# A four-layer attention and mixture-of-experts kernel: order of work in the second attention, and when the overflow slots run

## The chip, the cores and the metric

One core of a Trainium2 chip runs the whole program. Its engines work side by side, each through its own instructions in order: TensorE (PE in the profile, its weight loads PEld), VectorE (DVE), ScalarE (ACT), GpSimd (POOL), and SyncE (SP), which here only issues transfers. TensorE writes to PSUM; VectorE and ScalarE read it. The metric is the device time of one execution in microseconds (us), lower is better; the median of the runs is compared.

## The reference

Eight sequences of 256 tokens with 256 features pass four residual layers. The first mixes by correlation, the second is a balanced mixture of eight experts. The change touches the third and fourth:

```python
def _L1_xattn_ref(x, data, Wq, bq, Wkv, bkv, Wp, bp):
    ...
    q = (x @ Wq + bq).reshape(bs, n_ctx, HEADS, d)
    kv = (data @ Wkv + bkv).reshape(bs, n_data, HEADS, 2 * d)
    k, v = (kv[..., :d], kv[..., d:])
    scores = jnp.einsum('bqhd,bkhd->bhqk', q, k) * scale
    attn = jax.nn.softmax(scores, axis=-1)
    out = jnp.einsum('bhqk,bkhd->bqhd', attn, v).reshape(bs, n_ctx, WIDTH)
    return out @ Wp + bp

def _L1_ffn_ref(hidden_states, gate_W, w1_e, w3_e, w2_e, w1_s, w3_s, w2_s):
    ...
    probs = jax.nn.softmax(logits, axis=-1)
    top_v, top_i = jax.lax.top_k(probs, K)        # K = 2 of E = 8 experts
    g = jax.nn.silu(jnp.einsum('td,edf->etf', flat, w1_e))
    u = jnp.einsum('td,edf->etf', flat, w3_e)
    out_e = jnp.einsum('etf,efd->etd', g * u, w2_e)
    routed = jnp.einsum('te,etd->td', gates, out_e).reshape(b, s, d)
    ...                                           # and a shared expert
    return alpha * shared + (1.0 - alpha) * routed

x = x + _L1_xattn_ref(_layernorm(x, axis=-1), ctx_1024, ...)
x = x + _L1_ffn_ref(_layernorm(x, axis=-1), ...)
```

Everything is in float32: B = 8 sequences (called batches), S = 256 tokens, D = 256 features, 16 heads of 16, F = 1024 hidden features.

## The kernel before

Tokens lie on the 128 partitions, two tiles of 128 for a batch (TPB = 2); features are in two halves of 128 (KC = 2, and NB = 2 groups of eight heads). The whole program is written out in one order: each engine executes its instructions in the order in which the code issues them, and waits come from the tiles that they read and write.

**The second attention** (lines 2968 to 3054) runs over (b, c): batch b, group of heads c. One step holds two sets of `scores` (one for each 128 keys, `kt` 0 and 1). Each set is four products into two PSUM buffers of 128x1024 (pool `ps_s`, two buffers) and two exponentials on ScalarE that empty them. `values` of the step before are multiplied between the first and the second set, and `keep` copies them out on VectorE. Work of other batches is put between these:

- `turn_q(b+1)`, c = 0: turns the normalised rows of the next batch by four TensorE transpositions, and VectorE copies them from PSUM to `hT`.
- `queries(b+1, c)`: four products of `hT`, then two copies of the result into `QM`, each with one half of the heads masked out: the first on ScalarE, the second on VectorE.
- `turn_back(b-1)`: transposes the kept values, and VectorE divides by the sums of the softmax.
- `add_y(b+2)`, `batch_stats(b+2, "q")`: the residual and the statistics of a later batch. The statistics run on VectorE; the inverse root (`pow` and four small operations) on POOL.
- `turn_out(b-1)`, `project_out(b-1)`, c = 1: the output product and residual of the batch before. `norm_q(b+2)` normalises a later batch, one tile on VectorE and, from b = 2 on, the other on POOL; `add_bias` runs on POOL.
- `batch_stats(b-2, "m")`, `norm_m(b-2)`, c = 0: normalise the finished rows for the fourth layer; the normalisation is two POOL instructions. `turn_m(b-2)`, c = 1, turns them.

Copies to and from PSUM of all helpers share the pool `ps_m` with three buffers.

**The router** is the generator `route(g)` for four tiles (two batches): its pieces are issued one by one by `next(gates)`, three times in each (b, c), from batch 4 on. Piece 1 (issued when it is made) computes the logits; 2 turns them and takes the exponential on ScalarE; 3 to 5 pick the two largest on VectorE; 6 counts by two products with a triangular matrix and ones; 7 sums the counts (VectorE, `run`, line 2868); 8 yields the addresses. `send()` then scatters one row tile for one choice by an indirect transfer of POOL; sends wait for one another.

**The fourth layer** runs over blocks of 512 tokens: two shared blocks, eight experts, one shared. A block consists of four up units and one down unit (`run_unit`), on TensorE some 40 us. An expert takes its first 512 rows; more rows go to four slots of 32 rows (`slots()`, line 3616), a generator of which one piece is issued after most up units (`next(beside)`). It goes through F in four quarters (`q`): in one piece the way up (32 products of 32 columns each, line 3652, silu and product), in the next two transpositions, in the third the way down (16 products, line 3672) and, through `load_slots(q + 1)`, the transfers of the next quarter's weights: eight for the way up, four for the way down, 256 KB each, issued by SP. The piece with the last quarter's way down also loads the shared weights of the last block (`WS`). Between blocks, SP issues the weights of the experts and, in `take_apart` (line 3524), the transposing transfers of the rows of a block to come, which `join` (line 3530) puts together on ScalarE.

Of the kernel before, what the change touches and what calls it, by code (L numbers as in the profile page):

```python
# [19 lines left out]
P = 128  # L20
# [1066 lines left out]
def fast_path(  # L1087
# [1502 lines left out]
    def norm_q(b, *engs):  # L2590
        h2s[b] = hn.tile([P, TPB, D], F32, tag="h4", name="h2")
        batch_norm(b, "q", h2s[b], engs)
# [8 lines left out]
    def turn_pair(src, dst, copy):  # L2601
# [5 lines left out]
                )  # L2607
        copy(dst, pt.rearrange("p k j q -> p k (j q)"))

    def turn_q(b):  # L2610
        hTs[b] = pq2.tile([P, KC, S], F32, tag="hT", name="hT")
        turn_pair(h2s.pop(b), hTs[b], nc.vector.tensor_copy)

    def queries(b, c):
        if c == 0:
            QM[b] = pq2.tile([P, NB, 2, S], F32, tag="QM", name="QM")
        pp = ps_m.tile([P, S], F32, tag="pm", name="pp")
        for kc in range(KC):
            nc.tensor.matmul(
                pp,  # L2620
                wq[:, kc, c * P : (c + 1) * P],
                hTs[b][:, kc, :],
                start=(kc == 0),
                stop=(kc == KC - 1),
            )
        nc.scalar.activation(
            QM[b][:, c, 0, :],
            pp,
            AF.Identity,
            bias=bqm[:, c, 0:1],  # L2630
            scale=mask[:, 0:1],
        )
        nc.vector.tensor_scalar(
            QM[b][:, c, 1, :],
            pp,
            mask[:, 1:2],
            bqm[:, c, 1:2],
            ALU.mult,
            ALU.add,
        )  # L2640

    pex = at.enter_context(tc.tile_pool(name="pex", bufs=4))
    ex, pvs, ovs, ons, oTs = {}, {}, {}, {}, {}
# [305 lines left out]
        list(vals(i, 2, ps_m))  # L2949
    norm_q(0, nc.vector, nc.vector)  # L2950
    hTs[0] = pq2.tile([P, KC, S], F32, tag="hT", name="hT")
    transpose_tokens(h2s[0], hTs[0], ps_m, "pm", 0)
    nc.vector.tensor_tensor(bpb, bpb, pbp, ALU.add)
    queries(0, 0)
    queries(0, 1)
# [12 lines left out]
    for b in range(B):  # L2968
        for c in range(NB):
            scores(b, c, 0)  # L2970
            if (b, c) == (3, 0):
                router_weights()
            if prev:
                values(*prev, 0)
                values(*prev, 1)
                keep(*prev)
            send()
            if gates:
                next(gates, None)
            if prev is None:  # L2980
                list(vals(4, 1, ps_m, nc.vector.tensor_copy))
            elif b == 0:
                turn_q(1)
                norm_q(2, nc.vector, nc.vector)
                queries(1, 0)
                queries(1, 1)
            elif c == 0:
                if b + 1 < B:
                    turn_q(b + 1)
            else:  # L2990
                turn_out(b - 1)
                if 2 < b + 2 < B:
                    norm_q(b + 2, nc.vector, nc.vector if b < 2 else nc.gpsimd)
                    add_bias(b + 2)
            scores(b, c, 1)
            if gates:
                next(gates, None)
            if c == 0 and b >= 2:
                batch_stats(b - 2, "m")
                norm_m(b - 2)  # L3000
            send()
            if gates:
                next(gates, None)
            if c == 0:
                if b >= 1:
                    turn_back(b - 1)
                if 0 < b and b + 1 < B:
                    queries(b + 1, 0)
                    queries(b + 1, 1)
                if b + 2 < B and b:  # L3010
                    add_y(b + 2)
                    batch_stats(b + 2, "q")
                if b >= 4 and b % 2 == 0:
                    gates = route(b // 2 - 2)
                    next(gates)
            else:
                if b >= 2:
                    turn_m(b - 2)
                if b >= 1:
                    project_out(b - 1)  # L3020
                else:
                    add_bias(2)
            if prev is None:
                list(vals(5, 1, ps_m, nc.vector.tensor_copy))
                ct_scope.close()
                wsp = ctx.enter_context(tc.tile_pool(name="wsp", bufs=1, side="right"))
                pg1 = ctx.enter_context(tc.tile_pool(name="pg1", bufs=1, side="right"))
# [24 lines left out]
            if (b, c) == (1, 0):  # L3052
                router_columns()
            prev = b, c
# [4 lines left out]
    NQ = 4  # L3059
# [537 lines left out]
            for g in range(SLOTS)  # L3597
        ]

    def load_slots(q):  # L3600


        fs = slice(q * FQ, (q + 1) * FQ)
        wab = wsp.tile([P, 2, SLOTS, KC, FQ], F32, tag="wab", name=f"sab_{q}")
        wc = wsp.tile([P, SLOTS, FQ // P, D], F32, tag="wc", name=f"sc_{q}")
        wa, wb = wab[:, 0], wab[:, 1]
        for w, src in ((wa, L1_ffn_w1_e), (wb, L1_ffn_w3_e), (wc, L1_ffn_w2_e)):
            for g, e in enumerate(experts):
                part = src[bass.ds(e, 1)]
                part = part[:, fs, :] if w is wc else part[:, :, fs]  # L3610
                nc.sync.dma_start(
                    out=w[:, g], in_=part.rearrange("o (c p) d -> p (o c) d", p=P)
                )
        return wa, wb, wc

    def slots():

# [5 lines left out]
            in_=Td,  # L3623
            in_offset=bass.IndirectOffsetOnAxis(ap=rows_u, axis=0),
        )
        w = load_slots(0)
        yield
        gate = pg1.tile([P, 1], F32, name="gate")
        junk = pg1.tile([P, E], F32, name="junk")
# [14 lines left out]
        nc.vector.tensor_copy(RT, pt)  # L3644
        yield
        py = ps_v.tile([P, D], F32, tag="pv", name="pys")
        for q in range(NQ):
            pgu = ps_m.tile([P, 2, FQ], F32, tag="pm", name="pgu")
            for i in range(2):
                for kc in range(KC):  # L3650
                    for g in range(SLOTS):
                        nc.tensor.matmul(
                            pgu[g * SR : (g + 1) * SR, i, :],
                            RT[:, kc, g * SR : (g + 1) * SR],
                            w[i][:, g, kc, :],
                            start=(kc == 0),
                            stop=(kc == KC - 1),
                            skip_group_check=True,
                        )
            a = pe2.tile([P, FQ], F32, tag="as", name="as", bufs=1)  # L3660
            nc.scalar.activation(a, pgu[:, 0, :], AF.Silu)
            nc.vector.tensor_tensor(a, a, pgu[:, 1, :], ALU.mult)
            yield
            pt = ps_m.tile([P, FQ // P, P], F32, tag="pm", name="pt")
            for fi in range(FQ // P):
                nc.tensor.transpose(pt[:, fi, :], a[:, fi * P : (fi + 1) * P], ident)
# [3 lines left out]
            for fi in range(FQ // P):  # L3670
                for g in range(SLOTS):
                    nc.tensor.matmul(
                        py[g * SR : (g + 1) * SR, :],
                        aT[:, fi, g * SR : (g + 1) * SR],
                        w[2][:, g, fi, :],
                        start=(q == 0 and fi == 0),
                        stop=(q == NQ - 1 and fi == FQ // P - 1),
                        skip_group_check=True,
                    )
            if q + 1 < NQ:  # L3680
                w = load_slots(q + 1)
            else:
                WS = load_l1(wsp, -1)
                Y = pe2.tile([P, D], F32, tag="Ys", name="Ys", bufs=1)
                nc.scalar.activation(Y, py, AF.Copy, scale=gate)
                for g in range(SLOTS):
                    add_rows(Y[g * SR : (g + 1) * SR, :], ids[:, g : g + 1])
# [252 lines left out]
```

## Time and profile before

| | |
|---|---|
| runs, us | 823.51, 822.27, 825.11, 822.15 |
| median, us | 822.89 |
| profiled execution, us | 820.12 |
| its span, first to last instruction, us | 818.4 |
| granted TensorE clock | 0.999 |
| transfers | 109.59 MB, mean 134 GB/s |

The page gives the busy time and its share of the span for each engine. A timeline row holds: start from the beginning of the span, duration of the merged group, engine, line, operation, tile written and tiles read, shape, number of instructions, and in brackets the idle time of the engine before it with what ended it. Busy time by stretches, in us:

| stretch | length | PE | DVE | ACT | POOL |
|---|---|---|---|---|---|
| 200 to 222 | 22 | 21.22 | 6.10 | 7.17 | 3.06 |
| 222 to 238 | 16 | 13.64 | 10.50 | 10.25 | 5.93 |
| 238 to 254 | 16 | 16.00 | 8.13 | 10.65 | 3.86 |
| 286 to 302 | 16 | 15.33 | 13.08 | 11.17 | 8.38 |
| 302 to 318 | 16 | 14.51 | 10.53 | 9.12 | 9.98 |
| 318 to 334 | 16 | 16.00 | 9.78 | 11.57 | 8.29 |
| 334 to 350 | 16 | 15.76 | 7.49 | 6.65 | 10.59 |
| 510 to 530 | 20 | 20.00 | 13.30 | 9.38 | 4.68 |

The second attention lies from 222 to 342 us, the slots' products from 515 to 651 us.

### The profile page before, as it was taken

What the parts mean: (1) busy time and instruction counts of PE and PEld (TensorE: products, weight loads), DVE (VectorE), ACT (ScalarE), POOL (GpSimd) and SP (SyncE); (2) the same over time, 40 slices, a digit from 0 to 9 for tenths busy, and PEclk for the clock granted to TensorE, in tenths of its full rate; (3) what the DMA queues carried; (4) which work ended last, traced back from release to release, by engine and by line L of the source; (5) the groups of instructions that cost most, each with busy time, mean ns of one, the idle gap of its engine ahead of it and who ended that gap; (6) DMA issues with size and microseconds to landing.
All of it is one profiled execution on the core that took longest, in us unless ns stands there. A gap on an engine that the chain in (4) does not pass through costs nothing. (4 is left out here: it accounts for less than half of the span.)

```text
span 818.4 us, 13790 instructions
## 1 busy us (share of the span) xinstructions
PE 793.9 (97%) x5124; PEld 627.9 (77%) x5124; DVE 519.0 (63%) x1470; ACT 361.9 (44%) x672; POOL 216.7 (26%) x293
## 2 busy tenths in 40 slices
PE   8999999999999999999999999999999999999997
PEld 7546688778745555556899989797979798999986
DVE  6378877340456686555785777767676759586731
ACT  4344454324366666532334454444444544433330
POOL 6352122131125455552330000202020322112030
PEclk9999999999999999999999999999999999999999
DMA  8395567942160000142223485394949495411023
GB/s 264 90 289 177 170 202 224 323 156 91 42 178 27 15 1 24 38 164 90 71 69 79 132 261 156 84 297 96 287 100 302 90 317 113 136 14 20 7 40 120
DMA packets 104724, 109.59 MB, mean 134 GB/s; under 512 B 26408, under 2 KB 95240, under 8 KB 104616
## 3 DMA queue, kind: packets, MB, share of 16 engines
q1 hardware_dynamic: 95976, 95.30, 38.0%
q0 software_dynamic: 7920, 13.02, 7.4%
q8 instruction: 42, 0.69, 0.4%
q10 hardware_dynamic: 752, 0.30, 0.1%
q14 instruction: 34, 0.28, 0.1%
HBM read 80.61 MB, written 25.37 MB: 129 GB/s over the span
## 5 line engine op out<-in xcount | busy, mean ns | idle before, releaser
L3536 POOL DMA_INDIRECT Od<-Y,ids x32 | 51.8, 1620 | 291.7 <-DVE Y L3361 100.1
L3221 ACT COPY B<-a 128x512 f32<-128x512 f32 (+1 forms) x54 | 28.6, 531 | 169.7 <-PE a L3233 133.7
L2660 ACT ACTIVATE ex<-p,scale 128x1024 f32<-128x1024 f32 x64 | 67.8, 1111 | 32.5 <-PE p L2652 31.7
L3233 PE MATMUL a<-T,HP 128*128 128x256 f32 x288 | 73.9, 379 | 0.0
L3233 PE MATMUL a<-RT,wab 128*128 128x256 f32 x256 | 66.7, 383 | 0.4 <-DVE cc L3083 0.4
L3083 DVE TENSOR_TENSOR cc<-e,s 128x512 f32<-128x512 f32 x44 | 30.4, 690 | 57.6 <-PE e L3233 57.6
L3083 DVE TENSOR_TENSOR act<-act 128x256 f32<-128x256 f32 (+1 forms) x120 | 61.4, 512 | 2.7
L2372 PE MATMUL ph<-RT,w 128*128 128x256 f32 x256 | 61.7, 389 | 0.8 <-ACT RT L2359 0.7
L2389 PE MATMUL py<-w,A 128*128 128x256 f32 x256 | 61.6, 388 | 0.0
L3233 PEld LDWEIGHTS a<-T,HP 128*128 128x128 f32 x288 | 54.0, 190 | 7.0
L2381 ACT ACTIVATE A<-ph,b1c 128x256 f32<-128x256 f32 x64 | 30.1, 473 | 53.9 <-PE ph L2372 46.6
L3233 PEld LDWEIGHTS a<-RT,wab 128*128 128x128 f32 x256 | 46.3, 190 | 9.2 <-DVE cc L3083 2.5
L2372 PEld LDWEIGHTS ph<-RT,w 128*128 128x128 f32 x256 | 45.3, 190 | 8.9 <-ACT A L2381 1.1
L2389 PEld LDWEIGHTS py<-w,A 128*128 128x128 f32 x256 | 46.6, 190 | 6.4
L2894 POOL DMA_INDIRECT Td<-HP,to x32 | 32.6, 1018 | 56.4 <-DMA Td<-HP,to 48.9
L2652 PE MATMUL p<-QM,KT 32*128 32x512 f32 x256 | 40.4, 640 | 1.7 <-ACT ex L2660 1.2
L3083 DVE TENSOR_TENSOR act<-act,cc 128x512 f32<-128x512 f32 x44 | 30.3, 689 | 16.9 <-ACT act L3267 16.7
L2399 POOL DMA_INDIRECT Yd<-Y,ids x16 | 15.8, 986 | 81.6 <-DVE Y L2398 48.8
L3248 ACT COPY s<-a 128x512 f32<-128x512 f32 x44 | 25.8, 587 | 20.0 <-PE a L3233 20.0
L3233 PE MATMUL e<-T,wab 128*128 128x256 f32 x128 | 32.9, 380 | 0.3 <-DVE T L3083 0.3
L3233 PE MATMUL e<-RT,HP 128*128 128x256 f32 x128 | 32.8, 379 | 0.0
L3233 PE MATMUL B<-RT,wab 128*128 128x256 f32 x128 | 32.8, 379 | 0.0
(522 smaller groups left out, 1726.6 us busy)
## 6 DMA issues: line engine op xcount, KB each, us to landing
w<-in_L_ffn_w_dram SPq DMA_DIRECT2D x16, 1024.0 KB
wab<-in_L_ffn_w_e_dram SPq DMA_DIRECT2D x16, 1024.0 KB
wc<-in_L_ffn_w_e_dram SPq DMA_DIRECT2D x8, 1024.0 KB
sab<-in_L_ffn_w_e_dram SPq DMA_DIRECT2D x32, 256.0 KB
R<-Td SPq DMA_DIRECT2D x8, 530.0 KB
sc<-in_L_ffn_w_e_dram SPq DMA_DIRECT2D x16, 256.0 KB
Td<-blank SPq DMA_DIRECT2D x2, 1590.0 KB
X<-in_x_dram SPq DMA_DIRECT2D x4, 512.0 KB
```

Source lines behind the costliest of these rows:

```text
L2372: nc.tensor.matmul(ph, w1[:, kc, f * P : (f + 1) * P], RT[:, kc, :], start=(kc == 0), stop=(kc == KC - 1),)
L2381: nc.scalar.activation(A[:, f, :], ph, AF.Gelu_apprx_tanh, bias=b1c[:, e, f : f + 1])
L2389: nc.tensor.matmul(py, A[:, f, r * P : (r + 1) * P], w2[:, f, :], start=(f == 0), stop=(f == NF - 1),)
L2399: nc.gpsimd.indirect_dma_start(out=Yd, out_offset=bass.IndirectOffsetOnAxis(ap=ids[:, r : r + 1], axis=0), in_=Y[:, r, :], in_offset=None,)
L2652: nc.tensor.matmul(ps[g // 2][:, g % 2].rearrange("p m q -> p (m q)"), KT[rows, c, k0 : k0 + P], QM[b][rows, c].rearrange("p m q -> p (m q)"),
L2660: nc.scalar.activation(e4[:, 2 * j : 2 * j + 2], ps[j], AF.Exp, scale=scale)
L2894: nc.gpsimd.indirect_dma_start(out=Td, out_offset=bass.IndirectOffsetOnAxis(ap=to[g][:, k, j : j + 1], axis=0), in_=HP[:, GT * g + j, :], ...
L3083: eng.tensor_tensor(out, a, b, op)
L3221: nc.scalar.copy(self.b[:, 0 : self.n], self.a[:, 0 : self.n])
L3233: nc.tensor.matmul(ps[:, m * HT2 : (m + 1) * HT2], self.w.get(m, left, self.k), self.x.part[right], start=start and m == 0, stop=True, ski ...
L3248: nc.scalar.copy(self.s2, self.a)
L3536: nc.gpsimd.indirect_dma_start(out=Od, out_offset=bass.IndirectOffsetOnAxis(ap=ids, axis=0), in_=Y, in_offset=None, compute_op=ALU.add,)
```

## The change

In the attention, the first batch's rows are turned by `turn_pair` with one PSUM buffer and two VectorE copies, instead of `transpose_tokens` with two buffers and a copy each on VectorE and ScalarE. The queries of batch 1 and `norm_q(2)` move from before scores(0,1,1) to behind them, and both masks of these queries run on VectorE. The first `next(gates)` of each step is issued behind `turn_q`, or behind `turn_out`, `norm_q` and `add_bias`, instead of ahead of them. `batch_stats(b-2, "m")` and `norm_m(b-2)` move behind the second `send()`, the third `next(gates)` and `turn_back`.

```diff
+    def in_two(dst, src):
+        for kc in range(KC):
+            nc.vector.tensor_copy(dst[:, kc], src[:, kc])
...
-    def queries(b, c):
+    def queries(b, c, eng=nc.scalar):
...
+        for m in range(2):
+            if m == 0 and eng is nc.scalar:
+                nc.scalar.activation(
...
+            else:
+                nc.vector.tensor_scalar(
...
-    transpose_tokens(h2s[0], hTs[0], ps_m, "pm", 0)
+    turn_pair(h2s[0], hTs[0], in_two)
...
             send()
-            if gates:
-                next(gates, None)
             if prev is None:
                 list(vals(4, 1, ps_m, nc.vector.tensor_copy))
             elif b == 0:
                 turn_q(1)
-                norm_q(2, nc.vector, nc.vector)
-                queries(1, 0)
-                queries(1, 1)
             elif c == 0:
...
                     add_bias(b + 2)
+            if gates:
+                next(gates, None)
             scores(b, c, 1)
             if gates:
                 next(gates, None)
-            if c == 0 and b >= 2:
-                batch_stats(b - 2, "m")
-                norm_m(b - 2)
             send()
             if gates:
                 next(gates, None)
+            if (b, c) == (0, 1):
+                queries(1, 0, nc.vector)
+                queries(1, 1, nc.vector)
+                norm_q(2, nc.vector, nc.vector)
             if c == 0:
                 if b >= 1:
                     turn_back(b - 1)
+                if b >= 2:
+                    batch_stats(b - 2, "m")
+                    norm_m(b - 2)
```

In the slots, `load_slots` is split into `load_slots_up` (eight transfers) and `load_slots_down` (four). The first way up stands alone; from then on the way down of a quarter and the way up of the next are issued in one piece. A quarter takes two pieces instead of three, so the slots end a block earlier, and with them the load of the last shared weights.

```diff
+        def way_up():
             pgu = ps_m.tile([P, 2, FQ], F32, tag="pm", name="pgu")
...
             nc.vector.tensor_tensor(a, a, pgu[:, 1, :], ALU.mult)
-            yield
+            return a
+
+        a = way_up()
+        wab = load_slots_up(1)
+        yield
+        for q in range(NQ):
             pt = ps_m.tile([P, FQ // P, P], F32, tag="pm", name="pt")
...
             if q + 1 < NQ:
-                w = load_slots(q + 1)
+                wc = load_slots_down(q + 1)
+                a = way_up()
+                if q + 2 < NQ:
+                    wab = load_slots_up(q + 2)
             else:
                 WS = load_l1(wsp, -1)
```

More of the change, by code (lines that the diff above doesn't have):

```diff
@@ L2625, in queries @@
             )
[L2626 to L2640, printed above, removed]
+        for m in range(2):
+            if m == 0 and eng is nc.scalar:
+                nc.scalar.activation(
+                    QM[b][:, c, m, :],
+                    pp,
+                    AF.Identity,
+                    bias=bqm[:, c, m : m + 1],
+                    scale=mask[:, m : m + 1],
+                )
+            else:
+                nc.vector.tensor_scalar(
+                    QM[b][:, c, m, :],
+                    pp,
+                    mask[:, m : m + 1],
+                    bqm[:, c, m : m + 1],
+                    ALU.mult,
+                    ALU.add,
+                )
     pex = at.enter_context(tc.tile_pool(name="pex", bufs=4))
@@ L3598, in slot_experts, with load_slots_up, load_slots_down @@
         ]
-    def load_slots(q):
+    def load_slots_up(q):
         fs = slice(q * FQ, (q + 1) * FQ)
         wab = wsp.tile([P, 2, SLOTS, KC, FQ], F32, tag="wab", name=f"sab_{q}")
-        wc = wsp.tile([P, SLOTS, FQ // P, D], F32, tag="wc", name=f"sc_{q}")
[L3606 to L3614, printed above, removed]
+        for m, src in enumerate((L1_ffn_w1_e, L1_ffn_w3_e)):
+            for g, e in enumerate(experts):
+                nc.sync.dma_start(
+                    out=wab[:, m, g],
+                    in_=src[bass.ds(e, 1)][:, :, fs].rearrange(
+                        "o (c p) d -> p (o c) d", p=P
+                    ),
+                )
+        return wab
+    def load_slots_down(q):
+        fs = slice(q * FQ, (q + 1) * FQ)
+        wc = wsp.tile([P, SLOTS, FQ // P, D], F32, tag="wc", name=f"sc_{q}")
+        for g, e in enumerate(experts):
+            nc.sync.dma_start(
+                out=wc[:, g],
+                in_=L1_ffn_w2_e[bass.ds(e, 1)][:, fs, :].rearrange(
+                    "o (c p) d -> p (o c) d", p=P
+                ),
+            )
+        return wc
     def slots():
@@ L3625, in slots @@
         )
-        w = load_slots(0)
+        wab, wc = load_slots_up(0), load_slots_down(0)
         yield
@@ L3646, in slots @@
         py = ps_v.tile([P, D], F32, tag="pv", name="pys")
-        for q in range(NQ):
+        def way_up():
             pgu = ps_m.tile([P, 2, FQ], F32, tag="pm", name="pgu")
@@ L3654, in slots @@
                             RT[:, kc, g * SR : (g + 1) * SR],
-                            w[i][:, g, kc, :],
+                            wab[:, i, g, kc, :],
                             start=(kc == 0),
@@ L3674, in slots @@
                         aT[:, fi, g * SR : (g + 1) * SR],
-                        w[2][:, g, fi, :],
+                        wc[:, g, fi, :],
                         start=(q == 0 and fi == 0),
```

## The prediction

> **What bounds the kernel now.** The page first: TensorE is busy nearly everywhere, and the chain that ended last names only the final addition, so the time is TensorE's own row and the question is where that row has holes.
>
> ```profile
> PE 793.9 (97%) x5124; PEld 627.9 (77%) x5124; DVE 519.0 (63%) x1470; ACT 361.9 (44%) x672; POOL 216.7 (26%) x293
> ```
>
> Next the busy time by stretches. Attention (222 to 342 us) idles 4.8 us; from 490 to 810 us TensorE idles nowhere, so there only fewer or cheaper TensorE instructions count. Then the timeline of TensorE, start and length in us, last the idle time before. The first hole belongs to the queries of the second batch (L2619):
>
> ```profile
> 230.81 0.66 PE L2605 MATMUL pt<-ident,h 128*128 128x128 f32 x4
> 232.29 1.99 PE L2619 MATMUL pp<-hT,wq 128*128 128x256 f32 x8 [0.82 <-DVE hT L2608]
> 234.21 1.14 PE L2652 MATMUL p<-QM,KT 32*128 32x512 f32 x8
> 236.55 2.13 PE L2652 MATMUL p<-QM,KT 32*128 32x512 f32 x8 [1.20 <-ACT ex L2660]
> 238.62 1.93 PE L2669 MATMUL pv<-ex,VA 128*32 128x256 f32 x32
> ```
>
> TensorE waits for the turned rows, runs the queries, and then two sets of scores meet ScalarE's exponentials back to back; a set that takes 1.07 alone takes 2.07. The second hole, in batch 5, waits for the router's running counts on VectorE:
>
> ```profile
> 300.25 1.07 PE L2689 MATMUL pt<-ident,ov 128*128 128x128 f32 x8
> 303.19 1.97 PE L2619 MATMUL pp<-hT,wq 128*128 128x256 f32 x8 [1.86 <-DVE run L2868]
> ```
>
> I write times in this execution's clock; what has been won or lost before is left out of them.
>
> **Gains.** *The first rows.* Before, the second transposition of batch 0 waits 0.46 for ScalarE's copy of the values, and the queries' second half 0.55 for ScalarE's copy of hT. One bank and two VectorE copies of 0.42 (start about 0.34 apart) remove both; half of hT is there 0.15 to 0.47 sooner, depending on whether the first copy waits for two or four transpositions. I take **0.3**.
>
> *Second batch's queries.* Now scores(0,1,1) start at 231.4, right behind the transpositions (their banks are free at 229.9 and 230.95, the ends of the exponentials begun at 228.83). Queries follow at 232.5, hT being ready at 232.2. The first product reached its mask 1.17 after the queries' start before, so at 233.65; two masks of 0.54, 0.46 apart, end at 234.65. The exponentials of scores(0,1,1) run 232.6 to 234.7. scores(1,0,0) then start at 234.7 and the values at 235.8 instead of 238.62: **2.8**. If VectorE runs the masks at the 0.87 that each norm_q took beside POOL's add_bias (1.74 for two), and the second pair goes ahead, 1.6. norm_q(2), moved behind the masks, ends at about 236.3; turn_q(2) wants it at 237.7, so it is hidden; with under 1.4 of cover it would be paid. POOL's add_bias(2) waits behind it until 236.4 and nothing waits for that before 248.
>
> Both masks on one engine cost little by the trace: the VectorE mask began at 234.92, when ScalarE's (234.32, 0.56) was over, so the pair was already one after the other, 1.14 against 1.0. The Trainium skill, TensorEngine Tiling (Array Packing), section PSUM Bottleneck, says the opposite: empty PSUM with ScalarE and VectorE both. By that rule the split would be 0.5 us quicker and this part would win 2.3, the total being 823.0; I go by the row.
>
> *Batch 5's queries.* Turned rows now precede the router's step, statistics follow turn_back. The mask of picks ends at 300.5 instead of 299.9, so the counting products start at 300.6 (new wait 0.4), the counts end at 301.9 instead of 303.04, and the queries start at 302.05: **1.15** (0.9 if each VectorE step keeps a further 0.1 gap, 1.9 if nothing waits).
>
> *Slots.* No waits here; the price is that of changing the tile shape. Rows of a visit:
>
> ```profile
> 514.01 1.03 PE L3233 MATMUL a<-T,HP 128*128 128x256 f32 x4
> 514.96 1.93 PE L3652 MATMUL pgu<-sab,RTs 128*32 128x256 f32 x32
> 516.83 1.13 PE L3233 MATMUL a<-RT,wab 128*128 128x256 f32 x4
> 517.79 1.03 PE L3233 MATMUL e<-T,wab 128*128 128x256 f32 x4
> ```
>
> A group of four takes 0.864, so the visit of 32 costs 517.79 - 514.01 - 2 x 0.864 = 2.05. A visit of 16 (529.33, with 528.38 and 531.30 about it) costs 1.19. The difference is 0.86 for 16, so 0.33 of each visit is fixed. Eight visits become five (three joined; both products are 128*32): 3 x 0.33 = **0.95**; at least the visible entry and exit delays, 3 x 0.19 = 0.57. The transpositions, ScalarE's silu and VectorE's product are the same in number, in stretches where TensorE waits for nobody.
>
> SP's share: the weights keep their 3 MB a quarter, in two loads. The third quarter's up weights and second down weights now go out at about 564 to 571, ahead of the four transposing DMAs of take_apart, which were issued from 568.57. They landed by about 576; the join (L3530) wants them at 581.56, and 1.9 later under the change. 3.15 MB at the 281 to 309 GB/s seen at 576 to 582 take 11 us, to 575.5; 7.4 for the transposing, to 583. Zero, with the cover of ScalarE's place in its queue: TensorE needs the read behind the join about 2 us later still. The final shared weights come a block earlier.
>
> Gains: 0.3 + 2.8 + 1.15 + 0.95 = **5.2** (3.2 to 6.1).
>
> **Losses: the statistics behind turn_back.** VectorE and POOL of batch 2:
>
> ```profile
> 256.08 0.42 DVE L2562 BATCH_NORM_STATS2 b_st<-X 128x6 f32<-128x256 f32 x1
> ...
> 257.28 0.17 DVE L2565 TENSOR_SCALAR b_ve<-b_mv 128x2 f32<-128x2 f32 x1
> 257.35 0.25 DVE L2696 RECIPROCAL rs<-pt 128x16 f32<-128x16 f32 x1
> ...
> 258.26 0.42 DVE L2697 TENSOR_TENSOR on<-pt,rs 128x256 f32<-128x256 f32 x1
> ```
> ```profile
> 257.52 0.71 POOL L2567 TENSOR_TENSOR b_r<-b_ve,powers 128x2 f32<-128x2 f32 x1 [4.91 <-DVE b_ve L2565]
> ...
> 259.45 2.74 POOL L2581 TENSOR_SCALAR HP<-X,b_mv,b_r 128x256 f32<-128x256 f32 x2
> 262.59 0.72 POOL L2567 TENSOR_TENSOR b_r<-b_ve,powers 128x2 f32<-128x2 f32 x1 [0.40 <-DVE b_ve L2565]
> ...
> 264.23 0.20 POOL L2575 TENSOR_TENSOR b_r<-b_r,b_t 128x2 f32<-128x2 f32 x1
> ```
>
> Without statistics ahead, turn_back ends 2.03 after its first transposition (batch 1: 242.14 to 244.17). In batch 2 that is 258.43; statistics begin at 258.35 instead of 256.08. POOL's power starts 2.27 later, at 259.8, norm_m at 261.7, and ends at 264.15 with the 2.43 that the pair takes in batches 5 to 7, 264.46 with the 2.74 here. turn_m's second transposition came at 263.99. So TensorE waits about 0.35 (0.25 to 0.7) in **batch 2** and, one period on, **batch 3**. I take 2.43: the pairs of 2.74 had add_y (260.41, 0.68) inside their window, those of 2.43 had not, and add_y now falls ahead of norm_m. The Trainium skill, GPSIMD Engine Reference, section 1 Specifications, says that POOL contends with VectorE instructions that have two SBUF inputs, as add_y has. With it 2.43 would hold and the forecast be 822.5; with the batch's own row, three times 0.3 more, 823.4.
>
> **Batch 4** is worst. POOL's second chain, r1 of norm_q(6), ends 1.84 after norm_m, now at 294.8 instead of 293.17. The first router step used to run ahead of norm_q on VectorE; now it is behind:
>
> ```profile
> 292.47 0.19 DVE L2820 TENSOR_TENSOR lg<-pt,mx 128x32 f32<-128x32 f32 x1
> 292.57 0.68 DVE L2714 COPY oT<-pt 128x512 f32<-128x512 f32 x1
> 292.69 0.23 ACT L2822 ACTIVATE pr__3447<-lg 128x32 f32<-128x32 f32 x1 [0.76 <-DVE lg L2820]
> ```
>
> norm_q waits until 294.85, lg ends at 295.6, ScalarE's small exponential at 295.85, and only behind it the two of scores(4,1,1), 293.44 before. They end at 297.95; values(4,1) follow the second release by 1.07, at 299.0 instead of 296.67: **2.4** (2.1 to 2.7).
>
> **Batch 5** (L2689 brought forward): norm_m ends 0.45 late, but the 0.30 wait for oT there is gone; even. **Batch 6**: a send (1.0 on POOL, 2.7 apart by DMA) now stands ahead of the power: **0.25** (0 to 0.6). **Batch 7**: statistics from 334.65 instead of 332.22, norm_m ends at 340.5 instead of 338.05; turn_m stands at 338.69, so project_out starts at 341.05 instead of 339.59: **1.5** (1.2 to 1.8).
>
> Losses: 0.35 + 0.35 + 2.4 + 0.25 + 1.5 = **4.85** (3.8 to 6.5).
>
> **Forecast.** The profiled execution took 820.12 (span 818.4, 1.7 about it): 820.12 - 5.2 + 4.85 = 819.8. The median of the runs is 822.89, 2.8 above, so **822.5**; by the bounds (2.3 won to 3.3 lost) 820.6 to 826.2. Gains and losses nearly cancel.
>
> **Rivals.** *The POOL delay is hidden* (chance 0.19). If the norms reach turn_m and the router in time, only gains remain: 822.9 - 5.2 = 817.7. For it: 1.65 of slack in batch 2. Against it: the shift is 2.27, and batch 4's order is fixed by two queues.
> *Slot weights delay the transposing DMAs* (0.14), the slower side. If 3.15 MB move at 190 GB/s, between the mean of 134 and the 281 above, they end at 581, transposed rows land at 588.5, and the join stands in ScalarE's queue ahead of the read TensorE waits for (until about 585.5 free): 3 to 4 lost, 826.0. From that landing on each us costs one. Against it: this stretch moves more than 280.
> *The change doesn't do what it says* (0.12): masks at 0.87 leave 1.6, the tile shape's cost stays (0), so gains 3.05, losses 4.85: 824.7.
>
> **How the numbers follow.** Forecast 0.55. About 0.3% (2.5 us) is what a measurement of this kernel can tell from no change: faster means under 820.4, slower over 825.4. Faster: 0.17 of the hidden delay and 0.04 of the forecast; slower: 0.11 of the DMA rival, 0.04 of the third, 0.03 of the forecast; the rest, 0.61, the same. Range 818.6 to 826.2.
>
> **What would show it.** Right: values(0,1) some 2.8 sooner against scores(0,0,0); the wait of L2619 for L2868 down to about 0.4; in batch 4 ScalarE idle for about 3.5 ahead of L2822, which waits for VectorE behind L2581; turn_m (L2605, HP) waiting for POOL in batches 2, 3 and 7; L3672 and L3652 side by side. Wrong: no waits for POOL's L2581, or L3530 waiting for DMA.

## The result, and the profile after

The changed kernel takes 825.62 us (median of 45 runs, 821.19 to 833.18), the kernel before 822.15 (71 runs, 819.99 to 826.70). The ratio is 1.0043, 95% interval 1.0031 to 1.0054: about 3.5 us slower. I had forecast no difference. The profiled execution took 828.72, its span is 826.6, its granted clock 0.992 against 0.999. The profile before, 820.12, is one of the fastest executions of its kernel, so the two profiles are compared stretch by stretch below and not by their totals.

The engine row of the page first. TensorE has the same 5124 instructions; the span grew by 8.2, its busy time by 2.2, and that is instructions made longer by a lower clock: a second profile of the same kernel, at 0.997, has 793.5.

```profile
PE 796.1 (96%) x5124; PEld 630.1 (76%) x5124; DVE 520.6 (63%) x1473; ACT 359.7 (44%) x669; POOL 216.6 (26%) x293
```

**The gains came.** Timeline of TensorE (start, length, engine, line, operation, tiles, shape, count, and in brackets the idle time before it). The second batch's queries now stand behind scores(0,1,1), and values(0,1) start at 235.78 instead of 238.62. The first rows' gain did not come: from the last projection of the data (L1419, from 214.95 before and 214.82 after) to the first scores (222.19 and 222.13) it takes 7.24 us before and 7.31 after.

```profile
231.33 1.14 PE L2659 MATMUL p<-QM,KT 32*128 32x512 f32 x8
232.40 1.99 PE L2623 MATMUL pp<-hT,wq 128*128 128x256 f32 x8
234.71 1.14 PE L2659 MATMUL p<-QM,KT 32*128 32x512 f32 x8 [0.32 <-ACT ex L2667]
235.78 1.93 PE L2676 MATMUL pv<-ex,VA 128*32 128x256 f32 x32
```

The same view in batch 5 and in the slots. The wait for the counts is 0.36 (1.86 before), with a new one of 0.30 for the picks (`mk`, the mask of the chosen experts); a slot's way down (L3695) and the next way up (L3670) follow each other without a product of 128*128 between them.

```profile
303.50 0.18 PE L2859 MATMUL pc<-mk,ones_b 128*128 128x32 bf16 x1 [0.30 <-DVE mk L2855]
...
304.98 1.97 PE L2623 MATMUL pp<-hT,wq 128*128 128x256 f32 x8 [0.36 <-DVE run L2875]
```
```profile
538.53 1.07 PE L3695 MATMUL pys<-sc,aT 128*32 128x256 f32 x16
539.42 1.91 PE L3670 MATMUL pgu<-sab,RTs 128*32 128x256 f32 x32
541.26 1.13 PE L3241 MATMUL a<-RT,wab 128*128 128x256 f32 x4
```

**The losses came too, and larger.** The waits of TensorE from 222 to 400 us, summed (engine, tile and line that waits, the one waited for, us in total, times, longest). Before, no line of this view named POOL; now POOL's normalisation leads it, with 4.0 us in the batches and 3.4 behind the loop over batches, where the last rows and the first shared block run.

```profile
PE pt L2605 <- POOL HP L2581: 7.4, 8, 2.5
PE p L2659 <- ACT ex L2667: 1.9, 2, 1.5
PE p L2659 <- DVE QM L2640: 0.5, 1, 0.5
PE pp L2623 <- DVE run L2875: 0.4, 1, 0.4
PE pc L2859 <- DVE mk L2855: 0.3, 1, 0.3
```

What one batch costs is read from the starts of `project_out` (the product `pp<-wp,oT`), batch by batch. I worked the table out from such rows of each kernel's timeline: us from the first scores to the first output product (p0), then from each to the next; from the last (p7) to the product of L3794 in the fourth layer (L3768 before), from there to the first product of an expert, and the rest of the span. It leaves out what lies ahead of the first scores: 222.1 to 229.4 us in the profiles of this document, which follows no edit.

| kernel | p0 | p1 | p2 | p3 | p4 | p5 | p6 | p7 | to L3794 | to expert | rest | sum |
|---|---|---|---|---|---|---|---|---|---|---|---|---|
| before | 27.29 | 14.85 | 14.40 | 15.04 | 16.86 | 15.22 | 13.74 | 16.39 | 34.80 | 62.67 | 364.9 | 596.2 |
| changed | 24.52 | 15.60 | 15.14 | 15.09 | 20.24 | 15.93 | 14.95 | 16.28 | 40.09 | 62.67 | 364.0 | 604.5 |
| changed, 2nd profile | 24.52 | 15.61 | 15.14 | 15.08 | 18.61 | 15.83 | 14.94 | 16.29 | 34.80 | 62.67 | 363.8 | 597.3 |
| changed, 3rd profile | 24.52 | 15.60 | 15.15 | 15.08 | 18.60 | 15.94 | 14.94 | 16.29 | 34.79 | 62.67 | 363.8 | 597.4 |

The second and third profile (experiments 11 and 12) separate what the order costs every time from what came once. Every time: 0.75 in p1 and in p2, 1.75 in p4, 0.6 to 0.7 in p5, 1.2 in p6. Once: 1.6 more in p4 and 5.3 behind the loop.

**p1 and p2.** VectorE and POOL of batch 2, in order of time:

```profile
256.95 0.71 POOL L2567 TENSOR_TENSOR b_r<-b_ve,powers 128x2 f32<-128x2 f32 x1 [7.20 <-DVE b_ve L2565]
257.69 0.68 DVE L2553 TENSOR_TENSOR X<-X,yg 128x512 f32<-128x512 f32 x1
257.74 0.69 POOL L2572 TENSOR_TENSOR b_t<-b_r,b_ve 128x2 f32<-128x2 f32 x1
...
259.36 1.24 POOL L2581 TENSOR_SCALAR HP<-X,b_mv,b_r 128x256 f32<-128x256 f32 x1
```

POOL's L2572 of the same batch in the kernel before:

```profile
258.31 0.20 POOL L2572 TENSOR_TENSOR b_t<-b_r,b_ve 128x2 f32<-128x2 f32 x1
```

`norm_m` takes 2.43 for its pair, as forecast. But POOL's small product L2572 takes 0.69, not 0.20: it ends with `add_y` (L2553), which runs on VectorE beside it.

**p4.** ScalarE, VectorE and TensorE of batch 4, then the stretches around it (length, busy time of PE, PEld, DVE, ACT and POOL, granted clock, DMA share, GB/s):

```profile
294.63 0.23 ACT L2829 ACTIVATE pr__3457<-lg 128x32 f32<-128x32 f32 x1 [4.14 <-DVE lg L2827]
```
```profile
293.86 0.41 DVE L2581 TENSOR_SCALAR h<-X,b_mv,b_r 128x256 f32<-128x256 f32 x1 [2.29 <-POOL b_r L2575]
```
```profile
295.91 2.49 PE L2659 MATMUL p<-QM,KT 32*128 32x512 f32 x8 [1.54 <-ACT ex L2667]
298.33 3.22 PE L2676 MATMUL pv<-ex,VA 128*32 128x256 f32 x32
```
```profile
296.00:298.00 2.00, 2.00 (x8) 0.51 (x8) 1.79 (x7) 2.00 (x3) 0.65 (x1) 0.89 0.00 0
298.00:300.00 2.00, 2.00 (x18) 0.79 (x20) 0.83 (x3) 1.47 (x2) 0.00 (x0) 0.50 0.00 0
300.00:302.00 2.00, 2.00 (x24) 0.98 (x16) 0.38 (x1) 0.00 (x0) 0.00 (x0) 0.76 0.00 0
```

The chain is the one forecast: POOL's r1, VectorE's norm_q, the router's logits, ScalarE's small exponential, and only then the exponentials that TensorE waits for. Then the clock falls: the values take 3.22 where they took 1.93.

**Behind the loop.** POOL and TensorE from 354 us. Four sends stand in POOL's queue ahead of `norm_m(7)`; two of them wait 3.96 and 4.07 for the one before where 1.8 is usual. `turn_m(7)` waits, and the shared block's first products take 4.83 where 3.60 is usual.

```profile
357.49 0.97 POOL L2901 DMA_INDIRECT Td<-HP,to  x1 [1.81 <-DMA Td<-HP,to]
362.42 0.97 POOL L2901 DMA_INDIRECT Td<-HP,to  x1 [3.96 <-DMA Td<-HP,to]
367.46 0.97 POOL L2901 DMA_INDIRECT Td<-HP,to  x1 [4.07 <-DMA Td<-HP,to]
...
370.40 2.45 POOL L2581 TENSOR_SCALAR HP<-X,b_mv,b_r 128x256 f32<-128x256 f32 x2
```
```profile
371.69 0.33 PE L2605 MATMUL pt<-ident,HP 128*128 128x128 f32 x1 [2.49 <-POOL HP L2581]
372.91 0.90 PE L2605 MATMUL pt<-ident,HP 128*128 128x128 f32 x3 [0.89 <-POOL HP L2581]
373.61 4.83 PE L3203 MATMUL pgu<-HT,wab_-1_2725 128*128 128x512 f32 x8
```

### The profile page after: what moved, and what is told of

Read it like the earlier page. It is cut to its first block, busy times and chain, and to the rows that moved or that the text cites. A ratio compares the mean times of both kernels' runs of the same rounds, so it can differ in the third digit from the quotient of the medians.

```text
span 826.6 us, 13792 instructions
## 1 busy us (share of the span) xinstructions
PE 796.1 (96%) x5124; PEld 630.1 (76%) x5124; DVE 520.6 (63%) x1473; ACT 359.7 (44%) x669; POOL 216.6 (26%) x293
```

## The experiments

All ratios are to the kernel before, timed beside each kernel on the same chip; the columns are those of the table above.

| kernel | p0 | p1 | p2 | p3 | p4 | p5 | p6 | p7 | to L3794 | to expert | rest | sum | median | ratio, 95% interval |
|---|---|---|---|---|---|---|---|---|---|---|---|---|---|---|
| 1 statistics back | 24.52 | 14.84 | 14.40 | 15.04 | 17.17 | 15.04 | 13.69 | 16.29 | 41.14 | 62.67 | 364.1 | 598.9 | 823.24 | 0.9977, 0.9952 to 1.0001 |
| 2 router first | 24.52 | 15.61 | 15.16 | 15.10 | 16.75 | 15.80 | 15.28 | 16.28 | 34.79 | 62.67 | 363.8 | 595.8 | 824.32 | 1.0013, 0.9991 to 1.0036 |
| 3 slots alone | 27.29 | 14.84 | 14.40 | 15.04 | 16.85 | 15.14 | 13.74 | 16.38 | 34.79 | 62.67 | 363.9 | 595.0 | 822.93 | 0.9979, 0.9957 to 1.0002 |
| 4 queries alone | 24.52 | 14.85 | 14.40 | 15.04 | 16.87 | 15.19 | 13.75 | 16.38 | 34.81 | 62.66 | 365.0 | 593.5 | 822.04 | 0.9972, 0.9956 to 0.9989 |
| 5 statistics alone | 28.91 | 15.61 | 15.15 | 15.29 | 16.50 | 16.21 | 15.02 | 16.28 | 34.79 | 62.68 | 365.2 | 601.6 | 827.86 | 1.0041, 1.0020 to 1.0062 |
| 6 sends last | 24.52 | 15.61 | 15.14 | 15.09 | 18.62 | 16.24 | 14.95 | 16.29 | 34.78 | 67.74 | 364.0 | 603.0 | 830.95 | 1.0065, 1.0038 to 1.0091 |
| 7 counts first | 24.52 | 14.84 | 14.40 | 15.04 | 16.28 | 15.03 | 13.86 | 16.28 | 35.84 | 62.67 | 363.8 | 592.6 | 820.47 | 0.9949, 0.9921 to 0.9976 |
| 8 both, 6 and 7 | 24.51 | 14.85 | 14.40 | 15.03 | 16.29 | 15.03 | 13.77 | 16.28 | 34.79 | 64.79 | 364.1 | 593.8 | 823.21 | 0.9979, 0.9954 to 1.0003 |
| 9 masks split | 25.52 | 15.62 | 15.15 | 15.10 | 18.63 | 16.05 | 14.96 | 16.28 | 34.81 | 62.67 | 363.9 | 598.7 | 828.77 | 1.0036, 1.0019 to 1.0053 |
| 10 one send last | 24.52 | 14.84 | 14.41 | 15.04 | 16.29 | 15.04 | 14.26 | 16.28 | 34.81 | 62.68 | 363.9 | 592.1 | 820.78 | 0.9943, 0.9919 to 0.9968 |
| 11 changed again | 24.52 | 15.61 | 15.14 | 15.08 | 18.61 | 15.83 | 14.94 | 16.29 | 34.80 | 62.67 | 363.8 | 597.3 | 825.07 | 1.0029, 1.0010 to 1.0049 |

**1. The changed kernel with the statistics back in their old place.**

```diff
             send()
...
-                if b >= 2:
-                    batch_stats(b - 2, "m")
-                    norm_m(b - 2)
```
(and the three lines again ahead of the second `send()`)

> The changed kernel with batch_stats and norm_m of the finished rows put back ahead of the second send and of turn_back. Theory A (the statistics behind turn_back cause the loss): the waits of turn_m for POOL go (7.4 us in all after the change), the granted clock is 1.00 throughout, and the time is 2 to 5 us below the kernel before; of batch 5's 1.15 us gain most is given back. Theory B (the slots or their transfers cost it): the time stays 3 us above before.

The columns p1, p2, p5 and p6 return to the values of before, and p4 to 17.17: these losses are the statistics' move. What the move was for is undone with them: the queries of batch 5 wait 1.63 for the counts. But behind the loop 6.3 us are lost although the sends are as early as before (349.93; 350.12 before). So that loss does not need the move. Of theory A the waits came true in the batches (no wait for POOL in 2 to 6). The clock did not (0.93 from 350 to 400 us), nor is the time 2 to 5 us below before: 0.9977 cannot be told from no change.

**2. The changed kernel with the router's first piece ahead of `norm_q`.**

```diff
                 turn_out(b - 1)
+                if gates:
+                    next(gates, None)
                 if 2 < b + 2 < B:
                     norm_q(b + 2, nc.vector, ...)
...
-            if gates:
+            if gates and c == 0:
                 next(gates, None)
             scores(b, c, 1)
```

> The changed kernel with the first router piece of a c = 1 step right behind turn_out, ahead of norm_q. Theory A: ScalarE's idle time ahead of the router's exponential in batch 4 falls from 4.1 to under 1 us, scores(5,0,0) no longer wait, the values after them take 1.93 us instead of 3.22 because the clock stays at 1.00; 3 to 4.5 us won in the profile against the changed kernel, the waits for POOL in the other batches stay. Theory B (turn_m waits for POOL are all that matters): no change at batch 4 beyond 1 us.

p4 falls to 16.75, while p1, p2, p5 and p6 keep the changed kernel's values: batch 4's hole comes from the router's piece standing behind a `norm_q` that waits for POOL, and is a loss of its own. Theory A holds in the profile (1.9 us off p4 against the second profile, 3.5 against the first). In time the kernel is level with before.

**3 and 4. The kernel before with the joined slots alone, and with the second batch's queries, masks and `norm_q(2)` alone.** The edits are the parts of the change's diff.

> The kernel before with the joined slots alone. Theory A: three changes of the tile shape fewer, 0.95 us (0.57 to 1.0) faster than before. Theory B (the weights ahead of the transposing transfers delay join): 1 to 4 us slower, with ScalarE waiting for a transfer ahead of join.

> The kernel before with batch 1's queries, both masks on VectorE, and norm_q(2) behind scores(0,1,1), and nothing else. Theory A: 2.8 us faster than before, all of it between 230 and 239 us. Theory B (given back later in the attention, since ScalarE or POOL set the pace): under 1 us at the end.

The slots take 1.0 off the rest (363.9 against 364.9; forecast 0.95), too little for the runs to tell. The queries take 2.77 off p0 and touch no other column; the runs give 0.28% (0.11 to 0.44), that is 2.3 us.

**5. The kernel before with the statistics behind `turn_back`, alone.**

> The kernel before with one part of the change: batch_stats(b-2, m) and norm_m(b-2) behind turn_back; the router's pieces stay where they were. Theory A (turn_m pays for POOL): turn_m waits for POOL's L2581 in batches 2, 3, 5, 6 and 7 for 0.3 to 1.3 us each, 4 to 5 us together, and batch 4's scores(5,0,0) do not wait 1.5 us for ScalarE, since the router's piece stands ahead of norm_q again; 3 to 4.5 us slower than before. Theory B (the four sends behind the loop are the main loss, and come from the router's move): turn_m's waits are under 2 us, no more than 1 us slower.

Waits for POOL's L2581 of 4.2 us, ratio 1.0041: 3.4 us slower. The move alone costs about as much as the whole change, and batch 4 (p4 16.50) is free of the hole, since here the router's piece stands ahead of `norm_q`. Theory A. (p0, 28.91, holds a granted clock of 0.95 from 222 to 254 us; no edit touches it. The fall comes behind two waits of 0.82 and 1.20 us, which the kernel before has too.)

**6. The changed kernel with the four sends behind `norm_m(7)`.**

```diff
     norm_m(B - 2)
-    send(4)
...
     norm_m(B - 1)
+    send(4)
     next(gate2)
```

> The changed kernel with the four sends behind the loop issued behind norm_m(7). Theory A (these sends stand in POOL's queue ahead of norm_m(7) and wait beside the expert weights' loads): the wait of turn_m(7), 2.49 and 0.89 us in the changed kernel's profile, and the halved clock behind it, 1.2 us, are gone; 3 to 4.5 us faster than the changed kernel, so about 822, level with before. Theory B (the low clock there comes by itself and the wait varies with the runs): under 1 us faster than the changed kernel.

Theory A's gain did not come, and theory B's reason cannot be judged by this run (11 and 12 do). `turn_m(7)` no longer waits for these sends (34.78 to L3794), yet the kernel is slower, because the wait has moved. POOL issues the last 23 of 32 sends one behind the other, from 371.96 on; the last ends at 443.7, SP reads the first expert's rows behind it at 445.34, VectorE waits 9.03 for these, and TensorE for VectorE. TensorE's timeline there:

```profile
446.28 1.03 PE L3241 MATMUL a<-T,SS 128*128 128x256 f32 x4
450.45 1.49 PE L3241 MATMUL a<-HT,wab_-1_2725 128*128 128x256 f32 x4 [3.14 <-DVE X L3323]
451.73 1.91 PE L3241 MATMUL e<-T,SS 128*128 128x256 f32 x4
453.43 1.56 PE L3241 MATMUL a<-HT,wab_-1_2725 128*128 128x256 f32 x4
```

5.07 us to the expert, with the half clock behind the idle time again (0.77, 0.50 and 0.87 in the slices of 2 us from 450 on). In the kernel before, SP read these rows at 424.92, and VectorE took them up at 433.54 without waiting. From the first scores the read comes at 205.2 in the changed kernel's second profile and at 218.6 here. So the sends are due on both sides: four of them ahead of `norm_m(7)` can delay it, and 13 us later is too late for the expert.

**7. The changed kernel with the router's counts first.** The third `next(gates)` stands ahead of the statistics, these ahead of `send()` and `turn_back`, and the first piece ahead of `norm_q` as in 2.

```diff
             scores(b, c, 1)
-            if gates:
-                next(gates, None)
+            for _ in range(2):
+                if gates:
+                    next(gates, None)
+            if c == 0 and b >= 2:
+                batch_stats(b - 2, "m")
+                norm_m(b - 2)
             send()
```

> The changed kernel with the statistics back ahead of the second send, the router's third piece of a step ahead of the statistics, and its first piece of a c=1 step ahead of norm_q. Theory A: turn_m's waits in batches 2 to 6 are under 1 us together, scores(5,0,0) do not wait for ScalarE, queries(6) wait under 0.7 us; 3 to 4.5 us faster than the changed kernel, 1.5 to 2.5 us faster than before, and turn_m(7) may still wait for POOL behind the sends. Theory B (the waits only change their place): level with the changed kernel.

Ratio 0.9949 (0.9921 to 0.9976), 4.2 us faster than before, more than the 1.5 to 2.5 expected. It keeps the gains (p0, and p4 below before's); of the losses 1.0 behind the loop is left, and the queries have a new wait of 0.8 for `turn_back`'s division (`on`). The waits of TensorE from 222 to 400 us:

```profile
PE pt L2605 <- POOL HP L2581: 1.2, 2, 0.8
PE pp L2623 <- DVE on L2704: 0.8, 1, 0.8
...
PE pp L2623 <- DVE run L2875: 0.4, 1, 0.4
PE p L2659 <- ACT ex L2667: 0.3, 1, 0.3
PE pc L2859 <- DVE mk L2855: 0.3, 1, 0.3
```

**8. The edits of 6 and 7 together.**

> Both edits of the two kernels ahead of this one together: the four sends behind norm_m(7), the counts' piece ahead of the statistics and these ahead of turn_back, the router's first piece ahead of norm_q. Theory A (two separate losses): their gains add, 5 to 7 us faster than the changed kernel, 3 to 4 us faster than before, about 819.5. Theory B (one loss seen twice, the late sends coming from the late statistics): no faster than the better of the two alone.

The gains do not add: 34.79 to L3794, but 2.1 lost at the expert. It is no faster than 7, as theory B had it, though not for its reason: here the edit itself makes the sends late.

**9. The changed kernel with the second batch's first mask on ScalarE.** `queries(1, c)` without its third argument.

> The changed kernel with ScalarE taking the first mask of the second batch's queries again, VectorE the second. The rule of splitting the emptying of PSUM between ScalarE and VectorE: masks ready sooner, from scores(0,0,0) to values(0,1) 0.5 us less than the 13.65 of the changed kernel, the rest the same. My row (the masks follow each other anyway, and ScalarE's now stands behind two exponentials of scores(0,1,1), 1.1 us each): values(0,1) 0 to 1.5 us later, 0 to 0.2% slower than the changed kernel, so 824 to 827.

Timeline of ScalarE, then of VectorE and of TensorE:

```profile
238.91 2.12 ACT L2667 ACTIVATE ex<-p,scale 128x1024 f32<-128x1024 f32 x2 [1.61 <-PE p L2659]
240.92 1.02 ACT L2632 ACTIVATE QM<-pp,bqm,mask 128x256 f32<-128x256 f32 x2
```
```profile
241.52 1.00 DVE L2640 TENSOR_SCALAR QM<-pp,mask,bqm 128x256 f32<-128x256 f32 x2 [2.94 <-ACT QM L2632]
```
```profile
242.12 1.14 PE L2659 MATMUL p<-QM,KT 32*128 32x512 f32 x8 [1.32 <-DVE QM L2640]
```

ScalarE's masks stand behind its two exponentials, and VectorE's behind ScalarE's. p0 is 25.52: 1.0 later than with both on VectorE. The median, 828.77, lies above the 824 to 827 that I expected, but the ratio (1.0036) is no other than the changed kernel's.

**10. Kernel 7 with the last of the four sends behind `norm_m(7)`.** `send(3)` for `send(4)`, and `send()` behind `norm_m(B - 1)`.

> The kernel with the counts' piece first and the router's first piece ahead of norm_q (820.47, ratio 0.9949 to before), and the fourth of the four sends behind the loop put behind norm_m(7). Theory A (norm_m(7) waits only for the last send, 360.10 to 361.07 there): turn_m(7)'s wait, 0.76 us there, is gone and the next tiles' sends are late by less than 2 us with no wait for an expert's rows; 0.5 to 1 us faster than that kernel, ratio to before 0.993 to 0.995. Theory B (what is sent later is paid where the experts' rows are gathered, as with all four behind): a wait of over 1 us for VectorE's X ahead of the first expert, ratio 0.996 or above.

34.81 to L3794 and no wait at the expert: theory A in the profile. In time it cannot be told from 7 (0.9943 and 0.9949). Either beats both kernels; 7 is the smaller edit.

**11 and 12. The changed kernel itself again.**

> The changed kernel itself once more, for a second profile. Theory A (the waits in the attention belong to the order of the instructions, the long wait of the sends behind the loop to chance): from the first scores to the last output product 136.3 to 137.8 us, that is 2.5 to 4.0 more than before, the same waits for POOL's L2581 in batches 2 to 7; behind it, to L3794, either 34.8 us (no long wait) or about 40. Theory B (the long wait belongs to the change): about 40 us again, with a wait of 3 us or more of turn_m(7). Ratio to before 1.002 to 1.006.

> The same kernel, a third profile. Theory A: the same waits in the attention to 0.1 us; behind it 34.8 or about 40 us, by chance. Theory B: about 40 us a third time.

POOL's timeline of 11 behind the loop:

```profile
357.73 0.97 POOL L2901 DMA_INDIRECT Td<-HP,to  x1 [1.81 <-DMA Td<-HP,to]
360.62 0.97 POOL L2901 DMA_INDIRECT Td<-HP,to  x1 [1.92 <-DMA Td<-HP,to]
363.32 0.97 POOL L2901 DMA_INDIRECT Td<-HP,to  x1 [1.74 <-DMA Td<-HP,to]
366.87 2.44 POOL L2581 TENSOR_SCALAR HP<-X,b_mv,b_r 128x256 f32<-128x256 f32 x2
```

Same order, no long wait, 34.80 and 34.79 to L3794; batch 4's hole is 1.55 and 1.54 as in the first profile, at the full clock. The execution of 12 took 823.65. So the waits in the loop belong to the order; the long sends and the fallen clock in batch 4 came in one profile of three. The first part of my expectation, 136.3 to 137.8 to the last output product, was just missed (136.02 and 136.12), because the first profile holds the 1.6 of the clock.

## Why the prediction was wrong

The forecast was a small difference of large terms. The large gains were right, and so were most places of the losses; the sum of the losses was not. Forecast against the second profile of the changed kernel:

| step of the prediction | forecast | measured | from |
|---|---|---|---|
| first rows | -0.3 | +0.06 | from L1419 to the first scores, 7.24 to 7.30 |
| second batch's queries | -2.8 | -2.77 | p0 |
| batch 2, batch 3 | +0.35 each | +0.76, +0.74 | p1, p2 |
| batches 4 and 5, with batch 5's queries | +2.4 + 0 - 1.15 | +1.75 | p4 |
| batch 6 | +0.25 | +0.61 | p5 |
| batch 7 | +1.5 | +1.20 | p6 |
| slots | -0.95 | -1.1 | rest |

Behind the first scores the forecast sums to -0.05 and this profile to +1.1 (597.3 - 596.2). The steps one by one:

- *First rows*: wrong, and small. The queries still wait for hT, 0.79: one tile is copied only when all four transpositions are done, so the "two or four" of my text was four. Even that case I had put at 0.15 sooner; the first copy starts 4.16 us after the start of L1419 and started 3.94 after it before.
- *Second batch's queries, batch 5's queries, slots*: right. The wait for the counts was forecast at 0.4 and is 0.36. (3 x 0.33 is 1.0 and not the 0.95 of my sum; 1.0 to 1.1 were measured.)
- *Batches 2 and 3*: the mechanism was right, the size not. I took 0.35 out of 0.25 to 0.7, with `norm_m` at 2.43; `norm_m` did take 2.43, but I left the other POOL instructions at their old lengths. L2572 takes 0.68 in four batches of every profile in which the statistics stand behind `turn_back` (the changed kernel three times, and experiments 2, 5, 6 and 9), and 0.20 in these batches of the others: 0.48 more, which is the miss. I had moved `add_y` out of `norm_m`'s window and not asked where it went. The Trainium skill, GPSIMD Engine Reference, section 1 Specifications, says that POOL contends with VectorE instructions that have two SBUF inputs. The trace agrees, one instruction earlier than where I applied it.
- *Batch 4*: right. From `project_out` to values(4,1) it took 2.90 before and takes 5.51 in the second profile: 2.6, forecast 2.4 (2.1 to 2.7).
- *Batch 5*: called even, and it costs 0.24: `turn_m` waits 0.54 for POOL, where 0.30 were waited for oT.
- *Batch 6*: a send stands ahead of the power, as forecast, but it first waits 1.78 for the send before it, and the power starts where it ends (323.63 + 0.97, 324.62 in the second profile). I had priced 0.25 of 0 to 0.6.
- *Masks*: I went by the row and against a rule. The Trainium skill, TensorEngine Tiling (Array Packing), section PSUM Bottleneck, wants PSUM emptied by both engines, which I had estimated at 0.5 quicker here; experiment 9 is 1.0 slower. The rule says nothing of what already stands in ScalarE's queue.
- *Rivals*: the POOL delay is not hidden (3.9 us of waits in the batches of the second profile). The slot weights delay nothing: the join shows no wait for a transfer. The change does what it says.

Two things were in no term. **The queue behind the loop**: I followed POOL's queue in the batches and stopped at the loop's end, where the same queue holds four sends ahead of `norm_m(7)` and 19 behind. **The clock**: I priced an idle TensorE at its idle time. The first profile lost 1.6 in p4 to the clock and 5.3 behind the loop to both, experiment 1 lost 6.3 behind it, and the other two profiles of the changed kernel nothing.

How much of the measured 3.5 us these two make is open. The order accounts for 1.1. Another 0.4 lies outside the span: an execution of the changed kernel takes 2.1 us longer than its span, one of the kernel before 1.7, and no run shows why. In experiment 11 (2.4 us, interval 0.8 to 4.0) that can be all, and none of its twelve executions took more than 3.0 above the shortest, so it is not that some of them paid the 1.6 + 5.3 of the first profile and others nothing. In the main comparison (2.6 to 4.4) some 2 us remain. That the clock takes them is not shown, because it falls in the kernel before too: the mean granted clock was 0.9948 over 47 executions of the changed kernel and 0.9951 over 106 of the kernel before, timed beside the experiments. Nor is it shown for the sends: they were long in two of the eleven profiles that have all four ahead of `norm_m(7)`.

So the step that failed is "Losses: 4.85". The order alone makes them about 6.1 (1.1 + 2.77 + 1.15 + 1.1). The terms that were too small are batches 2 and 3 (0.35 each, 0.75 measured), where a POOL instruction was left at its old length, batch 5 (0 and 0.24) and batch 6 (0.25 and 0.61), where the wait ahead of a send was left out; batch 7 was too large (1.5 and 1.20). On the other side the 0.3 of the first rows is missing. And nothing was put down for what a hole can set off behind it, 1.7 us of clock twice in the first profile. The two edits that lose hang on one chain, POOL's: the statistics' move starts it 2.26 us later in batch 2 (2.27 forecast), and the router's move puts ScalarE's exponentials behind it. Experiment 5 shows the first loss alone, 2 takes the second away, and 7, without either, is faster than before.

What stays open beside these 2 us is why a send sometimes takes twice as long, told in the last section. A delay of the late statistics by other means was not tried.

## What to carry to other kernels

Before moving the head of a chain back, follow every instruction of the chain at its new time and ask what runs beside it there; and follow the queue to its end, also past the loop. A wait in front of an engine that is the bottleneck costs its length and sometimes more, which speaks for the order with fewer holes where two sums are equal; no run here tests that. Where a step waits in an in-order queue (here `norm_q` for POOL), nothing that another engine is due to read should stand behind it: putting the small router steps ahead of that wait, and the statistics ahead of `turn_back`, turned a loss of 0.4% into a gain of 0.5%.

## What was not expected of the hardware

**The clock falls behind a short hole, but not always.** In the first profile 1.54 us without work in batch 4 were followed by granted clocks of 0.89, 0.50 and 0.76 in slices of 2 us: 0.22 + 1.00 + 0.48 = 1.70 us of clock, as much as 3.4 us at half speed. The same hole (1.55 and 1.54) in the second and third profile left the clock at 1.00. Behind 3.14 us in experiment 6 it was 0.77, 0.50 and 0.87, again about 1.7, and in experiment 5 0.77, 0.50 and 0.88 behind the kernel before's own 0.82 and 1.20. Twelve of the fourteen profiles also have such falls ahead of the first scores, at 10, 100 or 160 us for the most part, where no two orders differ. Each takes 1.7 us of clock, never less; one in experiment 1 takes twice that. The Trainium skill, TensorE: Matmul & The Clock Gate, Part 1, states a half clock after at least one idle window of about 3.4 us, and the full one after a busy window of that length, with windows that run freely. The length of the slow stretch agrees, and free windows would account for a fall that comes and goes; a fall behind 1.54 us does not agree with a whole idle window. No run here shows the windows.

**A POOL instruction of 0.20 us takes 0.68 beside a VectorE addition of two tiles**, though it covers only 128x2 values: in batch 2 it starts 0.05 after the addition and ends 0.06 after it.

**An indirect transfer sometimes lands 2 us late with the transfer engines nearly idle.** In the first profile the send of 357.49 was waited for 3.96. Its data moved at 359.0 to 359.8 but for three packets, which came at 360.8 to 361.8, behind a single 16 KB packet of the instruction queue at 360.0. In experiment 1 such a packet lies within the long wait too. In ten other profiles a packet of that kind also fell among these sends, and they were waited for 1.7 to 2.5. It is a candidate, not a cause shown. Once late, the next send meets the experts' weights (transfer share 0.9 to 1.1 from 364 us on) and waits 4.07; without the first delay the four are issued by the time these begin.
